# A wait for the fourth of a row of indirect transfers on GpSimd, in a two-layer model with routed experts

## The chip, the cores and the metric

The kernel runs on one core of one Trainium2 chip. The metric is the device time of one execution in microseconds (us). The engines are named as the profile names them: PE (TensorE, matmuls), PEld (its weight loads), DVE (VectorE), ACT (ScalarE), POOL (GpSimd) and SP (SyncE, which here only issues transfers). Every engine works through its own program in order and waits on semaphores; transfers raise semaphores when they land.

## The reference

The input is 8 sequences of 512 tokens with 128 numbers each. Two layers are applied, each with two residual branches on a layernorm of the stream:

```python
x = x + _L0_attn_ref(_layernorm(x, axis=-1), ...)   # a state-space scan over time
x = x + _L0_ffn_ref(_layernorm(x, axis=-1), ...)    # one linear map, chosen by gumbel noise
x = x + _L1_attn_ref(_layernorm(x, axis=-1), ...)   # delta rule, a scan with 16 heads of 8x8 state
x = x + _L1_ffn_ref(_layernorm(x, axis=-1), ...)    # 8 experts, the 2 best of each token
```

The last branch matters here. For every token a router picks 2 of 8 experts, and the branch is the sum of both experts' outputs (128 to 512, GELU, 512 to 128), each times its softmax weight:

```python
topk_w, topk_idx = jax.lax.top_k(probs, TOP_K)
mask = jax.nn.one_hot(topk_idx, NUM_EXPERTS, dtype=xf.dtype)
weights = jnp.sum(topk_w[..., None] * mask, axis=1)
h = jax.nn.gelu(jnp.einsum('te,ieh->tih', xf, w1) + b1)
out = jnp.einsum('tih,ihe->tie', h, w2) + b2
out = jnp.sum(out * weights[..., None], axis=1)
```

## The kernel before

**Tiles and groups.** The 4096 tokens are 32 tiles of 128. `SIZES` makes chunks of them (2, 4, 4, 4, 4, 4, 4, 4, 2), which pass through the stages one after another: the state-space scan and the linear map (`scanned`, `ssm_out`, `linear`), the delta rule (`delta_in`, `delta_rule`), the router (`route`), and the experts. `GROUPS` joins the chunks for the experts: 2 tiles, three times 8, then 4, and the last 2, which go through all experts without sorting (`every_expert`). While the experts of one group run, the scans of later chunks go on, so from about 200 us on all stages are mixed on every engine.

**The experts of a group** (`experts`, line 1615). The place of every token among the rows sorted by expert is worked out on DVE (`dest`). Then, in this order:

- `scatter` (line 1683): for every tile and each of its 2 choices GpSimd issues one indirect transfer that writes the tile's 128 rows of 512 bytes from SBUF (`xne`) to their places in a DRAM table (`places`). 60 of these in all.
- `load_rows` and `load_weights` (lines 1712 and 1724): SP reads blocks of 128 sorted rows (`xb`) and the block's first expert matrix (`w1b`, 256 KB each).
- `hidden_of` (line 1760) and `second` (line 1742): PE transposes the rows (`ph`, copied by ACT to `xbT`), multiplies them by `w1b`, ACT applies GELU into one of three buffers `hid`, PE multiplies by the second matrix (`po` or `in`), ACT copies the outputs of four blocks into `yb` (line 1797), and SP writes them to a DRAM table (`results`).
- lines 1810 to 1817: for every tile and each choice GpSimd issues one indirect transfer that reads the 128 rows back from `results` to `back0` or `back1`, 64 KB each. These are the gathers, 60 in all; a chunk of four tiles has eight.
- lines 1819 to 1826: in the groups before the last two, ACT multiplies each gathered tile by its weight (`back<-back`), and GpSimd adds `back0` and `back1`, four tiles at a time, to the residual (`fin`). Lines 1828 to 1832: in the group of 4 tiles, DVE does both at once, a tile at a time. SP writes the sum out.

The last two tiles run through all eight experts at the end of the program; their sums `acc` are also formed by DVE, which works on `fin` and `acc` in turn, and PE's banks come free when `acc` has been read.

**What sets the order.** Every call on `nc` is recorded as an operation (`Recorder`, line 305) with an estimated cost (`_cost`, line 354: for a GpSimd tensor operation of n elements per partition 0.22 + 0.0015 n us below 64, else 0.4 + 0.0017 n; an indirect transfer 1.27). `Plan` has a planner (`place`, `backward`) that lets at most `BURST` = 4 indirect transfers start in `WINDOW` = 6 us of its own estimate. But the list `ORDER` (line 383) holds a place for each of the 4796 operations, so `best` takes the order from that list and the planner does not run. `emit` (line 294) then issues the operations in this order, and GpSimd's are kept in program order by `keep_in_program_order`.

**The waits of indirect transfers.** A transfer waits for the data it reads and the buffer it writes. The transfers of GpSimd's queue use eight semaphores in turn, and each also waits until the last user of its semaphore has landed, which is the eighth transfer before it. Between scatters of one group the kernel declares that there is no dependence (`declare_no_dep`, line 1692), since each writes rows of its own.

Of the kernel before, what the change touches and what calls it, by code (L numbers as in the profile page):

```python
# [40 lines left out]
class Bank:  # L41


    def __init__(self, choice, owner=None, step=None):
        self.owner, self.step = owner or self, step
        if owner is None:
            self.users, self.index, self.choice = 0, None, choice
# [22 lines left out]
class Plan:  # L70
# [4 lines left out]
    def __init__(self, tc, banks):  # L75
        self.tc, self.hw, self.banks = tc, tc.nc, banks
        self.ops, self.seen, self.key, self.slack = [], {}, 0.0, 0.0
        self.tensor, self.vector, self.scalar, self.gpsimd, self.sync = (
            Recorder(self, e) for e in ("tensor", "vector", "scalar", "gpsimd", "sync")
        )  # L80
# [31 lines left out]
    def add(self, engine, emit, reads, writes, cost, lag=0.0, table=None, group=None):  # L112
        op = Op()
        op.engine, op.emit, op.cost, op.lag, op.table = engine, emit, cost, lag, table
        op.by_rows = engine == "gpsimd" and lag < 0
        op.key, op.slack = (self.key, len(self.ops)), self.slack
        op.after, op.begins, op.ends = set(), [], []
        for x in reads:
            self.depend(op, x, False)
        for x in writes:  # L120
            self.depend(op, x, True, group)
        for x in (*reads, *writes):
            if isinstance(x, Bank):
                if x.owner.users == 0:
                    op.begins.append(x.owner)
                if x.owner not in op.ends:
                    x.owner.users += 1
                    op.ends.append(x.owner)
        self.ops.append(op)
# [5 lines left out]
    def later(self, op, f):  # L135
# [4 lines left out]
        if f.engine != op.engine or op.lag < 0:  # L140
            wait += LAG[op.engine] + f.slack
        return wait
# [75 lines left out]
    def place(self):  # L218
# [15 lines left out]
        while len(order) < len(self.ops):  # L234
# [44 lines left out]
            for b in op.ends:  # L279
                users[b] -= 1  # L280
                if users[b] == 0:
                    banks[index[b]] = done + LAG[op.engine]
            for f in followers[op]:
                at = done
                if f.engine != op.engine or op.lag < 0:
                    at += LAG[op.engine] + f.slack
                f.ready = max(f.ready, at)
# [6 lines left out]
    def emit(self):  # L294
        kind = mybir.EngineType
        with self.tc.manual_schedule(engines={kind.PE, kind.DVE, kind.Activation, kind.SP}):
            for op, switch in self.best():
                if switch:
                    self.hw.scalar.preload_act_table_set(switch)  # L299
                made = op.emit()  # L300
                if op.engine == "gpsimd":
                    self.tc.keep_in_program_order(made)


class Recorder:
# [5 lines left out]
    def __getattr__(self, name):  # L311
        plan, engine = self.plan, self.engine

        def record(*args, group=None, cost=None, **kw):
            def walk(x):
                if isinstance(x, bass.IndirectOffsetOnAxis):
                    return [x.ap]
                return [x] if isinstance(x, (bass.AP, Bank)) else []

            named = [k for k in ("out", "dst", "accum_out") if k in kw]  # L320
            outs = [a for k in named for a in walk(kw[k])]
            if not named or named == ["accum_out"]:
                outs += walk(args[0])
            ins = [a for x in (args if named[:1] in (["out"], ["dst"]) else args[1:]) for a in walk(x)]
            ins += [a for k, x in kw.items() if k not in named for a in walk(x)]

            def emit():
                on = lambda x: x.on(plan.banks) if isinstance(x, Bank) else x
                method = getattr(getattr(plan.hw, engine), name)
                return method(*(on(x) for x in args), **{k: on(x) for k, x in kw.items()})  # L330

            table = next((SETS[x] for x in args if isinstance(x, AF) and x in SETS), None)
            sizes = [_size(x) for x in outs + ins if not isinstance(x, Bank)]
            n = max([f for _, f in sizes], default=512)
            if "dma" in name:
                whole = min(p * f for p, f in sizes[:2]) if "indirect" not in name else sizes[0][0] * sizes[0][1]
                took, lag = (1.27 if engine == "gpsimd" else 0.42), -4.0 * whole
            else:
                took, lag = _cost(engine, name, n, kw), 0.0
                if ALU.pow in args:  # L340
                    took = 0.4 + 0.155 * n
            plan.add(engine, emit, ins, outs, took if cost is None else cost, lag, table, group)
# [29 lines left out]
PERIOD = 15.0  # L372
BEHIND = 8.0
BURST, WINDOW = 4, 6.0
LAG = {"tensor": 0.4, "vector": 0.3, "scalar": 0.3, "gpsimd": 0.3, "sync": 0.3}


# [261 lines left out]
def seq_kernel(  # L639
# [66 lines left out]
    def bank(name):  # L706
        return psum.tile([P, N], F32, tag=name, name=name)

    shared = [bank(f"po{i}") for i in range(2)] + [bank(f"in{i}") for i in range(2)]
    nc = Plan(tc, shared)  # L710
    own = {t: [bank(f"{t}{i}") for i in range(n)] for t, n in (("ph", 2),)}
# [24 lines left out]
    def ptile(shape, tag, bufs=1, dtype=F32):  # L736
        flat = turn(tag, bufs, lambda name: pipe.tile([P, WIDE.get(tag, N)], dtype, tag=name, name=name))
        return view(flat, shape)
# [62 lines left out]
    rows = ptile([n_rows, P], "hid", 3)  # L801
# [737 lines left out]
    def every_expert(g, x3T, weights, acc):  # L1539
# [47 lines left out]
    places = [  # L1587
        dram.tile([MAXB * P, D], F32, tag=f"places{i}", name=f"places{i}") for i in range(2)
    ]
# [25 lines left out]
    def experts(group):  # L1615
# [67 lines left out]
        def scatter(at, src):  # L1683
            def emit():
                rows_out = hw.gpsimd.indirect_dma_start(  # L1685
                    out=table[0 : nblk * P, :],
                    out_offset=bass.IndirectOffsetOnAxis(ap=at, axis=0),
                    in_=src,
                    in_offset=None,
                )  # L1690
                for before_ in scattered:
                    tc.declare_no_dep(rows_out.ins, before_, reason="every row has places of its own")
                scattered.append(rows_out.ins.name)
                return rows_out

            nc.add("gpsimd", emit, [at, src], [table], 1.27, -4.0 * P * D, group=(table.tensor.name, last))
# [324 lines left out]
```

## Time and profile before

| what | value |
|---|---|
| median of six runs | 648.17 us (646.32 to 649.99) |
| the profiled execution | 647.55 us |
| its span in the profile | 645.9 us |
| granted TensorE clock, mean | 0.92 |
| scatters on POOL | 60, 59.8 us busy |
| gathers on POOL | 60, 58.5 us busy |
| gathers, start to landing, where the profile has both | 2.7 / 3.4 / 6.1 us (least, median, most) |
| scatters, the same | 2.2 / 2.9 / 4.1 us |
| results of the last blocks to `results` | issued at 613.97, landed 2.70 later |
| gathers of the last group | start 617.53 to 626.30 |
| last sum `acc` of DVE | 639.73 |

All times in the text are us from the start of the span. [...] Rows of the timeline give start, duration, engine, line, operation, output and inputs, shapes, and in square brackets the engine's idle time just before and what ended it; "issue" there means that nothing the profile shows was waited for. Line 330 is a helper through which all recorded operations pass, so operations are told apart by their tiles' names. The chain that ended last is followed back from the last instruction to whatever released each step.

### The profile page before, as it was taken

How to read it: one execution, taken by the hardware profiler on the slowest of the kernel's cores; microseconds unless marked ns; L12 is line 12 of the kernel's file. 1: busy time of each engine (PE TensorE's matmuls, PEld its weight loads, DVE VectorE, ACT ScalarE, POOL GpSimd, SP SyncE). 2: the span in 40 equal slices, each digit the busy share in tenths (PEclk: the TensorE clock that was granted, in tenths of full speed). 3: DMA queues.
4: the chain of work that ended last, by engine and by line, in shares of the span. 5: the costliest groups of instructions: out<-in, count | busy, mean ns of one | idle time of the engine just before them, and what ended most of it. 6: DMA issues, size and time to landing. Idle time of an engine off the chain costs nothing.

```text
span 645.9 us, 10937 instructions
## 1 busy us (share of the span) xinstructions
PE 523.1 (81%) x3077; PEld 408.0 (63%) x3077; DVE 464.2 (72%) x1290; ACT 468.7 (73%) x984; POOL 458.1 (71%) x603
## 2 busy tenths in 40 slices
PE   3885668878778579888688798799987899889995
PEld 3652333544635446666377577578886799788884
DVE  7666238899988999998899999899997187001121
ACT  2875797978967568998899997975866567275631
POOL 6544466868758766989997797888668968845640
PEclk9998777979778789979899989799997999999999
DMA  4948234433434366366667556689977789678741
GB/s 133 329 133 263 78 91 119 125 83 98 119 92 114 99 175 168 91 175 181 183 176 200 151 158 192 174 236 219 245 197 203 219 247 268 197 231 243 233 144 41
DMA packets 96721, 110.16 MB, mean 171 GB/s; under 512 B 10179, under 2 KB 68206, under 8 KB 96662
## 3 DMA queue, kind: packets, MB, share of 16 engines
q1 hardware_dynamic: 91984, 101.31, 56.5%
q0 software_dynamic: 3904, 8.00, 4.4%
q8 instruction: 26, 0.43, 0.3%
q14 instruction: 33, 0.27, 0.1%
q10 hardware_dynamic: 774, 0.15, 0.1%
HBM read 85.90 MB, written 27.48 MB: 176 GB/s over the span
## 4 chain that ended last, share of the span: by engine, by line
DVE 36%; PE 20%; ACT 14%; POOL 11%; issue 6%; DMA 4%; POOLq 0%; DVEq 0%; ACTq 0%; SPq 0%
DVE st L330 18%; PE in L330 9%; DVE so L330 7%; PE ph L330 5%; POOL places L1685 4%; ACT f L330 3%; PE po L1747 3%; DVE prod L330 3%; ACT L299 2%; ACT b L330 2%; POOL back L330 2%; PE po L330 2%; POOL so L330 1%; ACT hid L330 1%; DMA back<-results,small_dest 1%
## 5 line engine op out<-in xcount | busy, mean ns | idle before, releaser
L330 PE MATMUL ph<-xbT,w1b 128*128 128x128 f32 x760 | 140.3, 285 | 8.2 <-ACT hid L330 3.7
L330 PEld LDWEIGHTS ph<-xbT,w1b 128*128 128x128 f32 x760 | 113.1, 198 | 14.7 <-ACT hid L330 5.4
L330 ACT ACTIVATE hid<-ph 128x512 f32<-128x512 f32 x111 | 65.6, 598 | 61.9 <-PE ph L330 45.9
L1747 PE MATMUL po<-w_sb,hid 128*128 x536 | 104.5, 286 | 0.4 <-DVE small_besti L330 0.4
L330 DVE TENSOR_TENSOR so<-kq,st 128x512 f32<-128x512 f32 x128 | 87.6, 685 | 6.1 <-DVE st L330 0.8
L1747 PEld LDWEIGHTS po<-w_sb,hid 128*128 128x128 f32 x536 | 84.7, 200 | 10.0 <-issue 7.9
L299 ACT ACT_TABLE_LOAD x64 | 82.1, 1283 | 8.9 <-DMA x<-in_L_attn_u_dram 7.8
L330 POOL DMA_INDIRECT back<-results,small_dest x60 | 58.5, 976 | 21.0 <-issue 13.5
L1685 POOL DMA_INDIRECT places<-xne,small_dest x60 | 59.8, 997 | 18.5 <-issue 10.8
L330 DVE TENSOR_REDUCE st<-st 128x64 f32<-128x320 f32 x128 | 63.6, 497 | 3.7
L330 DVE TENSOR_REDUCE st<-so 128x32 f32<-128x320 f32 x128 | 62.8, 490 | 3.9 <-ACT so L330 0.8
L330 PE MATMUL po<-wo,so 128*128 128x128 f32 x240 | 48.7, 307 | 10.5 <-POOL so L330 8.3
L330 DVE TENSOR_TENSOR st<-kq,st 128x256 f32<-128x256 f32 x128 | 54.5, 426 | 3.5
L330 PEld LDWEIGHTS po<-wo,so 128*128 128x128 f32 x240 | 40.8, 216 | 25.4 <-POOL so L330 11.0
L330 PE MATMUL in<-b,wqkvb 128*128 128x512 f32 (+1 forms) x72 | 39.7, 642 | 11.5 <-ACT b L330 3.6
L330 PE MATMUL in<-f,wT 128*128 128x512 f32 (+1 forms) x72 | 40.1, 650 | 8.1 <-DVE small_best L330 3.7
L1747 PE MATMUL in<-w_sb,hid 128*128 x224 | 44.2, 281 | 1.1 <-DVE st L330 1.0
L330 DVE TENSOR_TENSOR prod<-tmat,st 128x128 f32<-128x128 f32 x128 | 36.3, 284 | 7.4 <-POOL tmat L330 4.2
L330 DVE TENSOR_REDUCE st<-prod 128x32 f32<-128x128 f32 x128 | 37.2, 291 | 5.6 <-ACT upd L330 1.0
L330 POOL TENSOR_TENSOR f<-f,f 128x512 f32<-128x512 f32 (+1 forms) x27 | 32.3, 1197 | 12.4 <-ACT f L330 12.2
L330 POOL TENSOR_TENSOR so<-so 128x512 f32<-128x512 f32 x24 | 31.3, 1305 | 10.8 <-DVE so L330 8.3
L1747 PEld LDWEIGHTS in<-w_sb,hid 128*128 128x128 f32 x224 | 34.1, 191 | 2.3 <-issue 1.7
(339 smaller groups left out, 1358.7 us busy)
## 6 DMA issues: line engine op xcount, KB each, us to landing
kq<-scratch SPq DMA_DIRECT2D x64, 512.0 KB
w1b<-w1b_dram SPq DMA_DIRECT2D x103, 256.0 KB
xb<-places SPq DMA_DIRECT2D x20, 256.0 KB
results<-yb SPq DMA_DIRECT2D x20, 256.0 KB
places<-yb SPq DMA_DIRECT2D x2, 1472.0 KB
kq<-in_L_ffn_w_dram SPq DMA_DIRECT2D x2, 1024.0 KB
w1b_dram<-kq SPq DMA_DIRECT2D x2, 1024.0 KB
u_rows<-in_L_attn_u_dram SPq DMA_DIRECT2D x7, 256.0 KB
```

The source lines that it names most:

```text
L299: self.hw.scalar.preload_act_table_set(switch)
L330: return method(*(on(x) for x in args), **{k: on(x) for k, x in kw.items()})
L1685: rows_out = hw.gpsimd.indirect_dma_start(out=table[0 : nblk * P, :], out_offset=bass.IndirectOffsetOnAxis(ap=at, axis=0), in_=src, in_off ...
L1747: return hw.tensor.matmul(out_.on(nc.banks), lhsT=src, rhs=w2_f[:, bass.ds(at + c * P, P)], start=(c == 0), stop=(c == NHB - 1),)
```

## The change

While the operations are issued, the plan keeps a row: the names of the indirect transfers that GpSimd has been given since the last long operation. An operation of GpSimd whose estimated cost is over 0.6 us (a tensor operation of about 128 elements per partition or more) empties the row. When the row holds four transfers and the next operation of GpSimd's is a transfer again, that one is made to wait until the fourth has landed, and a new row begins with it. The wait stands in GpSimd's own program, so what follows it there waits as well. For scatters, the declaration that there is no dependence leaves out the one that is to be waited for.

```diff
+        self.row, self.to_land = [], None
...
             for op, switch in self.best():
                 if switch:
                     self.hw.scalar.preload_act_table_set(switch)
+                self.to_land = self.row[-1] if op.by_rows and len(self.row) == ROW else None
                 made = op.emit()
-                if op.engine == "gpsimd":
-                    self.tc.keep_in_program_order(made)
+                if op.engine != "gpsimd":
+                    continue
+                self.tc.keep_in_program_order(made)
+                if self.to_land:
+                    wait = mybir.DependencyInfo(mybir.DependencyClass.Sync, mybir.DependencyReason.DATA)
+                    self.tc.add_manual_dep(made.ins, self.to_land, wait, reason="short rows of indirect transfers")
+                    self.row = []
+                if op.by_rows:
+                    self.row.append(made.ins.name)
+                elif op.cost > 0.6:
+                    self.row = []
...
+ROW = 4
...
                 for before_ in scattered:
-                    tc.declare_no_dep(rows_out.ins, before_, reason="every row has places of its own")
+                    if before_ != nc.to_land:
+                        tc.declare_no_dep(rows_out.ins, before_, reason="every row has places of its own")
```

## The prediction

> **What bounds the kernel now.** I read the page first, then the busy table by stretches, then GpSimd's (POOL's) timeline from 440 us on, where the programs of the two kernels differ, and last the chain that ends last. The page: PE has the most busy time, no engine is full over the whole span, and the 60 row gathers (`back<-results`) take GpSimd about 1 us each, mostly with nothing between them but their own issue.
>
> ```profile
> PE 523.1 (81%) x3077; PEld 408.0 (63%) x3077; DVE 464.2 (72%) x1290; ACT 468.7 (73%) x984; POOL 458.1 (71%) x603
> ...
> L330 POOL DMA_INDIRECT back<-results,small_dest x60 | 58.5, 976 | 21.0 <-issue 13.5
> ```
>
> The busy table (columns: stretch, its length, then busy us and instructions of PE, PEld, DVE, ACT, POOL; clock; DMA share; GB/s) shows which engine sets the pace where the gathers are:
>
> ```profile
> 440.00:480.00 40.00, 37.59 (x294) 34.00 (x292) 37.92 (x113) 30.23 (x65) 25.88 (x41) 1.00 0.87 225
> ...
> 580.00:592.00 12.00, 11.46 (x89) 10.03 (x87) 1.69 (x9) 5.42 (x13) 7.58 (x8) 1.00 0.88 264
> 592.00:600.00 8.00, 6.79 (x58) 6.48 (x58) 2.01 (x6) 6.83 (x15) 4.39 (x4) 1.00 0.67 195
> 600.00:613.00 13.00, 13.00 (x99) 12.10 (x100) 0.42 (x1) 6.80 (x18) 7.82 (x9) 1.00 0.82 240
> 613.00:631.00 18.00, 17.24 (x111) 15.14 (x109) 5.59 (x18) 6.92 (x12) 8.05 (x9) 1.00 0.44 130
> ```
>
> From 440 to 480 DVE and PE are both at 94 to 95%. From 580 on PE is the bound, with 13.00 of 13.00 us in one stretch. A stall of PE there is not made up: it moves the end.
>
> **What the change does to the programs.** Both kernels have every engine's instructions in the same order (the list ORDER is complete, so no planner runs). PE, DVE, ACT and SP wait for the same things. On GpSimd five gathers get one wait more, each for the gather just before it, and a few later waits that these imply fall away (counted as nothing, below 0.1 us). No scatter is touched, since never more than four of them stand in GpSimd's program without a wide tensor operation between. In the times of the trace of before the five are A 453.75, B 569.81, C 585.84, D 604.13 and E 622.55. Before, they start 0.30 us after the end of the one before:
>
> ```profile
> 584.59 0.94 POOL L330 DMA_INDIRECT back<-results,small_dest  x1 [0.30 <-issue]
> 585.84 0.95 POOL L330 DMA_INDIRECT back<-results,small_dest  x1 [0.30 <-issue]
> ...
> 621.30 0.94 POOL L330 DMA_INDIRECT back<-results,small_dest  x1 [0.30 <-issue]
> 622.55 0.95 POOL L330 DMA_INDIRECT back<-results,small_dest  x1 [0.30 <-issue]
> ```
>
> **The delay of each wait** is (start of the fourth + its time to landing + 0.30 us of issue) minus the old start. The tile's view gives the landing for those at 452.50 (6.1), 584.59 and 621.30; the last two read
>
> ```profile
> DMA to landing us min/median/max: 5.2/5.2/5.2
> DMA to landing us min/median/max: 3.4/3.4/3.4
> ```
>
> For B's and D's fourth I take the last of the 16 increments of their semaphores in the trace: 4.3 and 3.2. So A 452.50+6.13+0.30-453.75 = 5.2; B 568.56+4.28+0.30-569.81 = 3.3; C 584.59+5.21+0.30-585.84 = 4.3; D 602.88+3.16+0.30-604.13 = 2.2; E 621.30+3.41+0.30-622.55 = 2.5. Together 17.5 us on GpSimd. What reaches the end is less, stage by stage.
>
> [...]
>
> **A (DVE-paced).** Behind it on GpSimd stand the small `small_shiftb` (455.18), `base` (to 456.93), a 2.42 us wait for DVE, `so` (459.36), three gathers, `qkp`, `small_prob` (465.51), `small_taken` (466.79). GpSimd's idle 2.42 and 0.48 us swallow about half: `so` and all up to `small_prob` come 2.4 us later. PE's use of `so` is at 464.77, 4.1 us after it, so it is covered. ACT's `small_prob` moves from 467.42 to about 468.3, 0.8 us; DVE reads it at 468.55. I take 0.5 us; the bounds are 0 (covered by DVE) and 2.4 (the whole shift on DVE).
>
> **B.** It is the last of its row; behind it stand two `fin` additions at 573.16 and 578.41, waiting for ACT. The new landing is near 577.5 and ACT multiplies that tile at 577.86: 0, at most 0.9 (the first `fin` late; ACT has 0.95 us idle soon after).
>
> **C.** Three more gathers are queued behind it (587.09, 588.34, 589.59), then `fin` 594.97. ACT multiplies in its own order, in front of PE's GELU tiles:
>
> ```profile
> 589.88 0.40 ACT L330 ACTIVATE back<-back,small_weight 128x128 f32<-128x128 f32 x1 [1.49 <-DMA back<-results,small_dest]
> ...
> 591.91 0.98 ACT L330 ACTIVATE back<-back,small_weight 128x128 f32<-128x128 f32 x3
> 594.01 0.60 ACT L330 ACTIVATE hid<-ph 128x512 f32<-128x512 f32 x1 [1.11 <-PE ph L330]
> ```
>
> The first of the three at 591.91 reads the sixth gather. That now starts near 590.1+1.25 = 591.35 and lands, with the 3.4 that the tile's view gives as the median, at 594.75; three products (0.98) put `hid` at 595.8 instead of 594.01: **1.8 us**, after the cover of 1.11. PE stands still for it, as it already waited 1.20 us for a GELU tile at 599.92. Bounds from landings of 2.7 and 5.2: 1.1 and 3.6.
>
> **D.** Two gathers behind it (605.38, 606.63), then two `fin`. ACT reads the three at 608.04, 609.08 and 610.39, with `hid` at 608.59 and 609.90 between them, in the stretch where PE is never idle. Those products ran at most 0.5 us after landing, so 2.2 less that cover: **1.7 us** for the GELU tiles, PE, and the copy `yb` (612.98) that ends the group. Bounds 0 (PE has other work) and 3.0.
>
> **E.** Nothing but three gathers is behind it. DVE takes the eight results in order, between the sums that free PE's banks. The chain that ends last (start, us, what) runs through the last of them:
>
> ```profile
> 626.30 3.43 DMA back<-results,small_dest
> 630.03 0.35 DVE fin L330
> 630.38 0.53 DVE acc L330 x2
> 630.95 0.71 PE po L330 x4
> ```
>
> PE was already 0.67 us late there, so the whole delay counts: **2.4 us**. Bounds 1.2 (the eighth lands with the smallest time, 2.7 in place of 3.4, and one half us of cover) and 3.0 (a wait that starts 0.86 us after landing, as 617.53 did after `results<-yb`, in place of 0.30).
>
> **Sum:** 0.5 + 0 + 1.8 + 1.7 + 2.4 = 6.4 us, bounds 2.3 and 12.9. The profiled execution took 647.55 us (span 645.9 and 1.65 around it): 647.55 + 6.4 = 654.0. It lies 0.62 below the median of the six runs, from which the same sum would give 654.6.
>
> **Rivals.**
> 1. *Only the end counts.* A to D are covered: PE's program has matmuls of other blocks ready while a GELU tile is late, and its 1.20 us idle at 599.92 is a gap to fall into. Against it: ACT's order puts the products in front of the tiles. Then E alone: 647.55 + 2.4 = 650.0.
> 2. *Longer waits.* Each upper bound: 647.55 + 12.9 = 660.4. For it: the gathers from 448.64 landed late (6.1). Against: PE is not at the end of A and B.
> 3. *Faster, by less crowding.* A row of eight keeps four or more gathers in flight while SP's weight loads use the DMA engines (share 0.88 from 580 to 592). If short rows let them all land sooner, the gather of 5.2 us on the chain at 584.59 falls to 2.7, as at 601.63, and `results<-yb` from 2.70 to 2.07 at 613.97. That is 2.5 + 0.6 = 3.1 us, and it decides only if the waits then cost nothing, for which a fourth gather would have to land 0.95 us after its start (1.25 less 0.30); none was under 2.7. Time 647.55 - 3.1 = 644.5.
> 4. *It does nothing.* The waits might be met on arrival. The trace says otherwise for all five, by 2.2 us or more; only full cover could hide them: 647.6.
>
> **How the numbers follow.** 0.3% is about what a measurement can tell from no change, here 1.9 us. Chances: forecast 0.60 (0.02 of it below 0.3%), rival 1 0.14 (0.08 slower, 0.06 within), rival 2 0.10, rival 3 0.10, rival 4 0.06. So slower 0.76, same 0.14, faster 0.10. The range, 648.0 to 660.0, leaves out the faster case and the tails on both sides.
>
> **What would show it.** Five gathers in GpSimd's timeline should show idle times of about 5.5, 3.6, 4.6, 2.5 and 2.8 us (delay and 0.30) put down to a DMA of `back`; ACT's products after C should wait for a DMA, and the `hid` after them start 1 to 3 us later; the last gather should start about 2.5 us later against its group's first, and so the last `fin`. I am wrong if the landing times shrink once only four are in flight, if PE's busy share from 580 to 631 stays as it was with the end moved by E alone, or if A's shift reaches the `st` chain of DVE in full.

## The result, and the profile after

The changed kernel takes 653.67 us (median of 23 runs, 650.70 to 657.56), the kernel before beside it 648.46 (49 runs, 643.01 to 652.24): a ratio of 1.0083, 95% interval 1.0065 to 1.0101, or some 5.2 us more. The profiled execution of the changed kernel took 653.1 us, 5.55 more than that of before, and its span is 5.5 us longer. Ratios and intervals, here and below, leave out runs over 1.5% above the fastest of their kernel. Later runs, told below, gave the opposite sign on one chip, and this sign again on another.

From the profile's page, the span, the busy times and the group of the gathers (count, busy us and mean ns, then idle us before them and what ended most of it):

```profile
span 651.4 us, 10941 instructions
...
PE 527.6 (81%) x3077; PEld 410.8 (63%) x3077; DVE 465.1 (71%) x1290; ACT 468.7 (72%) x984; POOL 458.1 (70%) x603
...
L341 POOL DMA_INDIRECT back<-results,small_dest x60 | 58.6, 976 | 37.3 <-DMA back<-results,small_dest 17.7
```

The work is the same; the idle time before the gathers rose from 21.0 to 37.3 us, and its largest part, 17.7 us, now ends when a gather lands. GpSimd's timeline (start, us, what, idle before and its end) shows the five waits:

```profile
458.69 0.94 POOL L341 DMA_INDIRECT back<-results,small_dest  x1 [5.07 <-DMA back<-results,small_dest]
...
572.64 0.95 POOL L341 DMA_INDIRECT back<-results,small_dest  x1 [3.60 <-DMA back<-results,small_dest]
...
589.40 0.94 POOL L341 DMA_INDIRECT back<-results,small_dest  x1 [4.22 <-DMA back<-results,small_dest]
...
607.15 0.94 POOL L341 DMA_INDIRECT back<-results,small_dest  x1 [2.37 <-DMA back<-results,small_dest]
...
628.93 1.00 POOL L341 DMA_INDIRECT back<-results,small_dest  x1 [2.43 <-DMA back<-results,small_dest]
```

Behind C and D, ACT waits in its own order for a gather, and the GELU tile `hid` follows:

```profile
594.09 0.98 ACT L341 ACTIVATE back<-back,small_weight 128x128 f32<-128x128 f32 x3 [2.71 <-DMA back<-results,small_dest]
594.98 0.57 ACT L341 ACTIVATE hid<-ph 128x512 f32<-128x512 f32 x1
...
613.85 0.40 ACT L341 ACTIVATE back<-back,small_weight 128x128 f32<-128x128 f32 x1 [2.78 <-DMA back<-results,small_dest]
614.15 0.58 ACT L341 ACTIVATE hid<-ph 128x512 f32<-128x512 f32 x1
```

PE in the same execution stands still for those tiles:

```profile
595.61 0.49 PE L341 MATMUL ph<-xbT,w1b 128*128 128x128 f32 x2 [1.46 <-ACT hid L341]
...
614.78 0.49 PE L341 MATMUL in<-w_sb,hid 128*128 128x128 f32 x2 [2.09 <-ACT hid L341]
```

The chain that ends last still runs through the gathers of the last group (start, us, what), now through the seventh of them and not the eighth:

```profile
631.49 2.47 DMA back<-results,small_dest
...
633.99 0.36 DVE fin L341
...
635.54 0.34 DVE fin L341
635.88 0.53 DVE acc L341 x2
...
636.46 0.71 PE po L341 x4
```

The last line is the same four matmuls as at 630.95 in the kernel before: 5.5 us later.

**Where the 5.5 us arose.** I pair each instruction of after with the same one of before and subtract the starts. The difference on PE is +0.2 from 60 to 440 us, +0.9 from 474 to 485, up to +2.2 at 489, +0.7 at 492, -0.1 at 500, -0.4 to -0.6 from 520 to 590, +1.0 at 600, +1.6 at 610, +3.9 at 620 and +5.5 at 631. So A added 0.7 that was gone again, B nothing, C 1.6, and D and E the rest.

### The profile page after: what moved, and what is told of

Same layout as the page of the kernel before. It is cut to its first block, busy times and chain, and to the rows that moved or that the text cites. A ratio compares the mean times of both kernels' runs of the same rounds, so it can differ in the third digit from the quotient of the medians.

```text
span 651.4 us, 10941 instructions
## 1 busy us (share of the span) xinstructions
PE 527.6 (81%) x3077; PEld 410.8 (63%) x3077; DVE 465.1 (71%) x1290; ACT 468.7 (72%) x984; POOL 458.1 (70%) x603
## 5 line engine op out<-in xcount | busy, mean ns | idle before, releaser
L341 POOL DMA_INDIRECT back<-results,small_dest x60 | 58.6, 976 | 37.3 <-DMA back<-results,small_dest 17.7
L341 PEld LDWEIGHTS po<-wo,so 128*128 128x128 f32 x240 | 40.1, 212 | 24.7 <-POOL so L341 10.2
```

## The experiments

### One wait at a time

Of the five waits only one is kept in each of four kernels; the order stays. B, forecast at 0, was not run alone.

```diff
+                    if self.count in KEPT:
                         wait = mybir.DependencyInfo(...)
                         self.tc.add_manual_dep(made.ins, self.to_land, wait, ...)
+                    self.count += 1
...
+KEPT = (0,)   # only_a; (2,) only_c; (3,) only_d; (4,) only_e
```

> Of the five new waits only the first (A, at 453.75 us of the profile before) is left. Theory (each wait costs what its gather's landing delays in the order of ACT and DVE in front of PE): the gather starts about 5 us later, PE is 0.5 to 0.9 us late between 474 and 492, and because the profile after shows that lost again by 500, the time is 648.5 to 649.0 (before 648.5). Rival (all of GpSimd's delay comes through): 5.2 us, 653.7. Rival (E alone counts): 648.5, and no shift on PE between 474 and 492.

> Only the third wait (C, at 585.84 us before) is left. Theory: GpSimd's gather starts about 4.3 us later, ACT's product of the sixth gather and the GELU behind it come 1.6 to 1.8 us later, and so do all matmuls after 600: 650.1 to 650.3 (before 648.5). Rival (E alone counts): the delay is hidden, 648.5. Rival (all of GpSimd's delay comes through): 652.8. If C also is what made D's sixth gather land in 5.4 us instead of 3.7, the shift after 615 is larger than that at 600, by up to 1.3 us.

> Only the fourth wait (D, at 604.13 us before) is left. Theory as forecast: 1.7 us on the way to the end, 650.2 (before 648.5). The profile after shows 3.0 there, since the gather landed in 5.42 us against 3.67. Theory that this longer landing is D's own: 3.0 here too, 651.5. Rival (C's shift moved it into other traffic): the landing is 3.7 again and the cost 1.2 to 1.7, 649.7 to 650.2. Rival (E alone counts): 648.5.

> Only the fifth wait (E, at 622.55 us before) is left. Theory: the last gather starts 2.4 us later and the last sums on DVE with it: 2.4 us, 650.9, if that gather lands in 3.4 us as before; 1.6 us, 650.1, if it lands in 2.5 us as after. Rival (the last sums have slack, so that only C and D count): 648.5. Rival (E alone counts for the whole difference): 653.7.

Measured, on one chip, where the kernel before took 665.49 us (35 runs) and not 648:

| kernel | median us, 12 runs | ratio to before, 95% interval |
|---|---|---|
| only A | 666.39 | 1.0001 (0.9970 to 1.0032) |
| only C | 662.89 | 0.9960 (0.9930 to 0.9990) |
| only D | 664.79 | 0.9983 (0.9956 to 1.0009) |
| only E | 665.67 | 1.0000 (0.9970 to 1.0030) |

For C, D and E the forecast prices do not show: no wait costs anything that can be measured, and C alone makes the kernel a little faster. The times fit the rivals in which the delay stays hidden, but those contradict each other, since one lets E alone count and another E not at all. A agrees with its forecast, but no more than with nothing at all. As prices of single waits in the condition of the record these four are inconclusive, since the kernel before was 17 us slower here. That had to be found first.

### Which transfer is waited for, and how often

The first kernel waits for the first of the row instead of the fourth, the second has rows of two.

```diff
-                self.to_land = self.row[-1] if op.by_rows and len(self.row) == ROW else None
+                self.to_land = self.row[0] if op.by_rows and len(self.row) == ROW else None
```

```diff
-ROW = 4
+ROW = 2
```

> The changed kernel, but each of the five gathers waits for the first of its row in place of the fourth. In the profile before the first of the row had landed by then in B to E, and would land 2.3 us later in A. Theory (the price is the landing of the fourth): 648.5 to 649.0, as before, and no idle time of GpSimd ahead of B to E. Rival (a wait costs by itself, or splits the row, whatever it waits for): near the 653.7 of the changed kernel.

> The changed kernel with rows of two: a wait after every two indirect transfers, three waits in each group of eight gathers, and some among the scatters too. Theory: every wait stops GpSimd for about 2.4 to 5 us, so C, D and E delay their last gathers by three such waits each (7 to 13 us) instead of one, of which 2 to 3 us stay hidden at C and at D: 5 to 10 us at each of C, D and E, 665 to 678 us in all (before 648.5, after 653.7). Rival (less crowding): transfers that are alone land in under 2.5 us, the waits shrink and the time stays within 650 to 658.

Measured on a second chip, where the kernel before took 667.07 us (23 runs): first of the row 664.75 us (12 runs), ratio 0.9967 (0.9938 to 0.9996); rows of two 687.48 us (4 runs: 679.60, 683.55, 691.42 and 693.09), ratio on record 1.034 (1.0266 to 1.0414), where the two fastest alone give 1.022. In the trace of the first the gathers at C, D and E start 0.30 to 0.34 us after the one before has been issued (B 1.19, A 3.05): there the wait is met on arrival, and it costs nothing that this chip shows. The second is 20 us above the kernel before by the medians, and 14.5 us by the two fastest runs, where the theory had 17 to 30 above 648.5. That does not confirm the price of a stop: the kernel before is late here by something that rows of two almost do not have (below), and against 648.5 the two fastest runs are 31 and 35 us slower, more than the theory gave.

### The products on DVE

The 16 products of the gathered rows that stand behind C and D are taken out of ACT's order, in the kernel before and in the changed one.

```diff
-                        nc.scalar.mul(back[c][:, i], back[c][:, i], weights[:, c, i : i + 1])
+                        by = nc.vector.tensor_scalar_mul if last == LAST - 6 else nc.scalar.mul
+                        by(back[c][:, i], back[c][:, i], weights[:, c, i : i + 1])
```

> The kernel before, with the 16 products of the gathered rows by their weights of the fourth group (the gathers of the waits C and D) on DVE in place of ACT. Theory: little changes without the waits, since ACT waited there for landed gathers up to 1.7 us ahead of the GELU and DVE has some 1.5 us of idle time in each stretch of 8: 646 to 650. Rival (DVE's order in front of PE is as tight as ACT's): 651 to 655.

> The changed kernel with the same 16 products on DVE. Theory (C and D reach PE only through the products in ACT's order ahead of the GELU): ACT's GELUs of 594 and 611 to 614 no longer wait for a gather, the 4.6 us of C and D go from ACT's way, and what is left above the same edit of the kernel before is A's 0 and E's 1.6 to 2.4 us, plus up to 4.6 where DVE's sums wait behind the products instead. Rival (the delay reaches the end by GpSimd's own order): the difference to that kernel stays 5.4 us and ACT's GELUs stay late.

Measured on the same second chip: in the kernel before 664.43 us (8 runs; four more took 668.52 to 670.66), ratio 0.9956 (0.9921 to 0.9992); in the changed kernel 657.55 us (6 runs), ratio 0.9857 (0.9809 to 0.9906). So the waits made this form 6.9 us faster, where the theory had 1.6 to 7.0 us slower and the rival 5.4. Both fall here as forecasts of the time. In the trace of the changed form ACT's GELU tiles from 588 to 621 us no longer wait for a gather, as the theory said, though GpSimd still stops for 4.41 us at C. Something else than the waits' own price was at work, and it was on the side of the short rows.

### Both kernels once more, and what is late

> The changed kernel once more, unchanged, beside the kernel before on the same chip, since the eight runs above had the kernel before at 665.5 to 667.1 us and not at 648.5, and no single wait cost anything there. Theory (the price of C, D and E is there whatever else is late): 5 to 6 us above the kernel before. Rival (where the kernel before takes 665 us, signals from DMAs and PE reach ACT late anyway, and the gathers' delay hides behind that): within 2 us of the kernel before, or up to 4 us below it, as the single waits and the first-landed row were 0 to 2.7 us below.

> The kernel before, unchanged, for its profile on the same chip. If the kernel takes some 665 us here too: all of the extra 17 us lie behind 440 us, where ACT's GELU is seen to start up to 4 us after the last matmul that it needs. If it takes 648 us: the profile is that of before, and the earlier runs are to be told apart by their chips.

Measured on a third chip: the changed kernel 659.57 us (7 runs), the kernel before 665.79 (11 runs; one more took 674.16), ratio 0.9923 (0.9887 to 0.9958). The same two programs, with the other sign. (The execution of the changed kernel that was profiled, 665.16 us, is the slowest of its seven.)

The profiles say where the 17 us are. In the group of GELU tiles on the page, the idle time before them was 61.9 us in the record's kernel before and is here

```profile
L330 ACT ACTIVATE hid<-ph 128x512 f32<-128x512 f32 x111 | 65.5, 598 | 79.8 <-PE ph L330 43.2
```

and against the record's execution the span grows only behind 500 us. Take the stretch of C. ACT's timeline of the kernel before, on this chip ("remote" is a releaser of which the profile holds no record):

```profile
589.15 0.60 ACT L330 ACTIVATE hid<-ph 128x512 f32<-128x512 f32 x1 [2.29 <-remote]
594.26 0.60 ACT L330 ACTIVATE hid<-ph 128x512 f32<-128x512 f32 x1 [4.52 <-remote]
```

PE, where the first line holds the last matmuls for that second tile and the third line is what waits for it:

```profile
589.07 0.39 PE L330 MATMUL ph<-xbT,w1b 128*128 128x128 f32 x2
...
590.35 0.39 PE L330 MATMUL ph<-xbT,w1b 128*128 128x128 f32 x2
594.91 0.48 PE L330 MATMUL ph<-ident,xb 128*128 128x128 f32 x1 [4.18 <-ACT hid L330]
```

and GpSimd meanwhile:

```profile
582.67 0.96 POOL L330 DMA_INDIRECT back<-results,small_dest  x1 [1.27 <-DMA results<-yb]
...
587.69 0.94 POOL L330 DMA_INDIRECT back<-results,small_dest  x1 [0.30 <-issue]
588.94 0.95 POOL L330 DMA_INDIRECT back<-results,small_dest  x1 [0.30 <-issue]
590.19 0.94 POOL L330 DMA_INDIRECT back<-results,small_dest  x1 [0.30 <-issue]
591.44 0.94 POOL L330 DMA_INDIRECT back<-results,small_dest  x1 [0.30 <-issue]
```

The last matmul that the tile needs ends at 589.46 by its record. ACT is free, and starts at 594.26, after the whole row of eight has been issued; PE has nothing to do for 4.18 us. In the record the same tile started 0.1 us after its matmul (587.53). The changed kernel, same chip, same tiles:

```profile
593.13 0.60 ACT L341 ACTIVATE hid<-ph 128x512 f32<-128x512 f32 x1 [3.43 <-PE ph L341]
594.65 0.60 ACT L341 ACTIVATE hid<-ph 128x512 f32<-128x512 f32 x1 [0.93 <-PE ph L341]
596.15 0.60 ACT L341 ACTIVATE hid<-ph 128x512 f32<-128x512 f32 x1 [0.90 <-PE ph L341]
...
603.58 0.98 ACT L341 ACTIVATE back<-back,small_weight 128x128 f32<-128x128 f32 x3 [2.60 <-DMA back<-results,small_dest]
```

The tiles follow with 0.9 us between them, and the product behind C waits 2.60 us, as it does in the record (2.71). The price of C is there, and the wait of 4.52 us for the third of these tiles is gone (0.90).

To see this for all of them I took the 145 instructions of ACT and DVE that wait for PE in the record's kernel before, and measured in each trace how long each started after the recorded end of the matmul it needs (or after its engine came free). "Late" is over 0.3 us. In the record's kernel before they are picked so that none is; in the record's changed kernel none is either. They are sorted by how many indirect transfers GpSimd had begun in the 5 us before that matmul's end (and up to 0.3 after):

| trace | 0 to 2 begun | 3 begun | 4 or more | late in all, us |
|---|---|---|---|---|
| before, record | 0 late of 108 | 0 of 23 | 0 of 14 | 0 |
| after, record | 0 of 111 | 0 of 23 | 0 of 11 | 0 |
| before, third chip | 0 of 112 | 5 of 22 | 7 of 11 | 22.8 |
| after, third chip | 0 of 118 | 5 of 19 | 4 of 8 | 12.6 |
| rows of two, second chip | 1 of 130 | 1 of 14 | 1 of 1 | 2.6 |

The four kernels with one wait, on the first chip, have 14 or 15 late and 16.4 to 24.3 us; waiting for the first of the row, on the second, has 12 and 19.9. In the kernel before on the third chip the readers of PE are late only in the midst of a row of indirect transfers, and the more often the longer the row (0 of 112, 5 of 22, 7 of 11); rows of two on the second chip leave 3 late of 145. The changed kernel on the third chip has 10.2 us less of this lateness than the kernel before, against its own price of about 5.5: 4.7 us gained by this count, 6.2 by the medians. The count is an estimate, since not all of the lateness need lie on the way to the end. The two profiled executions themselves do not show the medians' gap (spans 663.5 and 661.7). Paired, the changed kernel is 3.3 us later from 200 to 300 us, where no gather waits, 6.3 at 580, 0.2 at 620 and 1.8 at the end: over C and D it gains 6.1 us, the reverse of the record, and E costs. In these traces records are missing too: of the landing signals of transfers 5,411 are recorded in the kernel before on the third chip, 7,333 in the record. Rows of two have 6,030, so records are missing also where hardly a reader is late.

The lateness is taken from the start of the reader. No run here separates an effect of the recording from a delay of the signals themselves.

### The changed kernel a third time, and a pause without a wait

In the second kernel GpSimd does five memsets of a spare tile, which nothing reads, in place of each wait.

```diff
+                if op.by_rows and len(self.row) == ROW:
+                    for _ in range(5):
+                        self.tc.keep_in_program_order(self.hw.gpsimd.memset(self.pad, 0.0))
+                    self.row = []
```

> The changed kernel unchanged, a third time, beside the kernel before and the pause on one chip. Theory (two conditions): if the profile shows ACT's GELU starting within 0.1 us of the last matmul that it needs, as in the record, the kernel before takes some 648 us and this one 5 us more. If it shows starts up to 4 us late behind rows of indirect transfers, as in the ten runs above, the kernel before takes some 666 us and this one 4 to 8 us less. Rival (the run that was 6.3 us below was a chance): within 2 us of the kernel before.

> The five waits are replaced by a pause of GpSimd at the same five places, five memsets of 128x512 of a tile of their own, some 2.5 us, that waits for no transfer; the order is otherwise that of the kernel before. Theory (what helps where signals come late is that GpSimd issues no row of more than four without a break, and what costs is the break): like the changed kernel, 2 to 6 us below the kernel before where that takes 666 us, 1 to 5 us above it where that takes 648 us. Rival (what helps is that the fourth transfer has landed, so that none is in flight): no gain, within 2 us of the kernel before or slower by the pause, where that takes 666 us.

Measured on a fourth chip, where the kernel before took 647.59 us (13 runs): the changed kernel 654.52 us (8 runs), ratio 1.0101 (1.0064 to 1.0138); the pause 654.21 us (6 runs), ratio 1.0104 (1.0057 to 1.0151). In both traces none of the 145 readers is late, and as many landing signals are recorded as in the record (7,357 and 7,349). So the record stands in its condition, and the theory of two conditions is confirmed for the changed kernel. By the medians the pause costs as much as the wait. GpSimd at C, in the kernel with the pause:

```profile
585.93 0.95 POOL L340 DMA_INDIRECT back<-results,small_dest  x1 [0.30 <-issue]
586.88 2.87 POOL L303 MEMSET pad<- 128x512 f32 x5
589.90 0.96 POOL L340 DMA_INDIRECT back<-results,small_dest  x1 [0.15 <-issue]
```

The fifth gather starts 3.97 us after the fourth instead of 1.25, 2.7 us late, and no transfer was waited for. So here the gathers that start later cost time (654.21 us against 647.59) also where no landing holds them. Place by place the two kernels differ, though. Paired with the record's kernel before, PE loses 0.2 us at C, 2.8 at D and 2.0 at E with the pause, and 1.6, 3.0 and 1.6 with the waits; at C the waits delay the fifth gather by 3.9 us and the pause by 2.7. The profiled pause (656.7 us, 2.5 above its median) also loses 1.2 us around 530, where PE waits for a weight transfer, and has two stretches at half the granted clock (555.0 to 558.4 and 636.9 to 643.7) that the kernel before does not have. The equal medians are in part chance. Whether the pause also helps where readers start late was not seen: this chip had none.

## Why the prediction was right, point by point

**The delays on GpSimd: right.** Forecast idle times 5.5, 3.6, 4.6, 2.5 and 2.8 us; measured 5.07, 3.60, 4.22, 2.37 and 2.43, and on the fourth chip 5.27, 3.56, 4.56, 1.79 and 2.25.

**A, 0.5 (0 to 2.4): right in place, but it did not last.** A made PE 0.7 us late (1.0 on the fourth chip) from 474 to 485, and at 500 nothing is left of it. Before `po<-wo,so` PE idles 3.44 us in before and 1.93 in after, and around it the granted clock differs. By windows (us, then busy time and count of PE, PEld, DVE, ACT, POOL, then PEclk, DMA share, GB/s), before:

```profile
488.00:491.00 3.00, 0.96 (x7) 0.72 (x6) 2.60 (x6) 2.97 (x6) 2.81 (x4) 1.00 0.96 293
491.00:494.00 3.00, 1.60 (x7) 1.60 (x8) 2.79 (x7) 1.86 (x6) 2.77 (x4) 0.53 1.04 244
494.00:498.00 4.00, 4.00 (x21) 4.00 (x20) 2.69 (x6) 0.00 (x0) 3.63 (x4) 0.50 0.45 113
```

and after:

```profile
488.00:491.00 3.00, 3.00 (x14) 2.82 (x13) 2.09 (x5) 2.95 (x6) 2.92 (x3) 0.50 1.03 340
491.00:494.00 3.00, 1.07 (x8) 0.78 (x8) 2.79 (x7) 2.76 (x8) 2.63 (x4) 0.95 0.93 222
494.00:498.00 4.00, 4.00 (x24) 4.00 (x24) 3.67 (x9) 0.00 (x0) 3.61 (x4) 0.59 0.71 180
```

By the trace's clock records the clock is at half from 491.17 to 498.00 in before, and from 487.90 to 491.31 and from 494.73 to 498.14 in after: as long in all. In after the first half falls on matmuls ahead of the idle time; it makes PE up to 2.2 us late at 489, and the idle time takes that up. Behind it the first matmuls run at full clock, where all those up to 498 run at half in before, and 24 in place of 21 are done between 494 and 498. The late stage catches up. The forecast had nothing of this.

**B, 0: right** (-0.4 before it, -0.6 after).

**C, 1.8 (1.1 to 3.6): right, with luck.** The sixth gather landed 3.42 us after its start (the forecast took 3.4, the median of all), the product waited, the tile came at 594.98, and PE's shift went from -0.6 to +1.0: 1.6 us. On the fourth chip 1.6 to 1.7. In before this gather took 4.63 us, by the last increment of its semaphore; with that the same sum would have given 3.0. Why the median should hold behind the wait, the forecast did not say.

**D, 1.7 (0 to 3.0): too small, and one of its two ways was missed.** The forecast followed the tiles. But D's products also feed `fin` on GpSimd, and SP issues `out_rows<-fin` in front of `results<-yb`, for which the last group's gathers wait. On the fourth chip this is plain, since there `yb` is ready early. GpSimd:

```profile
614.83 2.62 POOL L341 TENSOR_TENSOR fin<-fin,back 128x512 f32<-128x512 f32 x2 [3.79 <-ACT back L341]
621.53 0.96 POOL L341 DMA_INDIRECT back<-results,small_dest  x1 [4.09 <-DMA results<-yb]
```

ACT and SP in the same execution:

```profile
615.41 0.48 ACT L341 COPY yb<-po 128x384 f32<-128x384 f32 x1 [0.67 <-PE po L1760]
```

```profile
617.47 0.38 SPq L341 DMA_DIRECT2D out_rows<-fin  x1
617.95 0.45 SPq L341 DMA_DIRECT2D results<-yb  x1
```

`yb` is done at 615.89, `fin` at 617.45, and `results<-yb` leaves at 617.95, behind `out_rows<-fin`. `fin` started at 610.86 in before, at 615.10 in after and at 614.83 here: 4.24 and 3.97 us later, of which 0.95 and 1.97 were there on PE at 600. So D is 3.3 and 2.0 on the way to the last gathers. In after the sixth gather of D also took 5.42 us to land (3.67 in before).

**E, 2.4 (1.2 to 3.0): too large.** The wait delays the gather as forecast (2.43 us idle). But by then the first gather of the group is already 4.26 us late (621.79 against 617.53), and the end is 5.5 late: E adds 1.2, and on the fourth chip 5.8 - 4.0 = 1.8. The forecast let the last gather land in 3.43 us as before; it took 2.5. Four of the eight gathers of that group had landed in 2.46 to 2.58 us in before, by the last increments of their semaphores, so the smallest time of 2.7, from which the lower bound was made, was too long as well. The last gather starts 2.2 us later against its group's first, where 2.5 was forecast.

**The sum: 6.4 forecast, 5.5 and 5.8 in the two profiles.** In after that is -0.6 where C begins, 1.6, 3.3 and 1.2. D's miss (+0.3 and +1.6) and E's (-0.6 and -1.2) offset each other, so the total is better than its terms; that is luck.

**The rivals.** That E alone counts fell: C and D make up most of the 5.5 us. All upper bounds (660.4) and nothing (647.6) fell too. *Faster, by less crowding* is wrong in the record's condition, but its first half came true, and with it a sign that the prediction had named for being wrong: landing times did shrink. By the last increments on record the five gathers that now wait took 4.13 us to land on average in before and 2.80 in after (2.72 on the fourth chip), and the 13 from each wait to the end of its row 3.70 and 3.21 (3.01), with 5.42 in place of 3.67 for one at D. This was worth less than the stops cost. On the third chip the kernel was faster, but by another way than this rival's: it spoke of landing times, and what went down with short rows was the lateness of PE's readers, 12.6 us in place of 22.8.

**What stays open.** Three chips gave 665 to 667 us and late readers, a fourth 648 and none; for the record the chip is not known. Whether that is the chip, the time, or the recording of the profile is not settled, and neither is what holds the readers of PE in the midst of a row of transfers. The single prices of C, D and E in the condition of the record rest on two traces, not on kernels of their own. Rows of two were not run in that condition either. The form with the products on DVE and the waits (657.55 us, the fastest against its own kernel before) was run in the condition with late readers alone.

## What to carry to other kernels

Here five breaks in rows of GpSimd's transfers held it for 17.7 us, and the end came 5.5 us later. Follow a break through every reader in order, with the cover that each has, the output transfer that stands in front of another one in SP's queue included. Look, before trusting a small verdict, whether readers start right after the work they need: here the same change cost 0.8 to 1.0% where they did and gained 0.8% where they did not. Run both kernels beside each other on more than one chip before keeping it.

## What was not expected of the hardware

- In the table's three traces from the second and third chips, 23 of 75 readers of PE's results behind three or more indirect transfers begun within 5 us started late, one of them, at 594.26 in the kernel before, 4.5 us after its engine had come free and 4.8 after the recorded end of the matmul; with two or fewer begun, 1 of 360 was late. In the four traces of the first chip 14 or 15 readers were late, in the two of the fourth none.
- PE's granted clock was at half for stretches of 3.41 or 6.83 us around 490 us, and the stage behind A, 0.9 us late from 474 to 485 in after, stood at -0.1 us at 500, where part of the stretch had moved ahead of an idle time that took up what it cost. PE was busy for 0.35 of the 3.41 us before 491.17 in before, and for 0.43 of those before 487.90 and before 494.73 in after. It was busy for 0.59 of the 3.41 us before 487.76 in before, where the clock stayed full. That A's delay, by lowering this share, brought the first half forward fits these numbers, but was not tested.
- Moving the wait from landing to a fixed pause of 2.87 us changed the median by 0.3 us, though the two lose their time in different places: on the fourth chip, where no reader is late, the stop without a landing to wait for cost 6.6 us by the medians.
